# Splitting a layer norm and a router's choice into steps for later slots of an attention loop

## The chip, the cores and the metric

The kernel runs on one core of one Trainium2 chip. Its time is the device time of one execution in microseconds; the times given are medians of several executions.

## The reference

A block of attention and a mixture of experts, each with a residual and a layer norm without weights, in float32. There are four batches of 1024 tokens with 256 features.

```python
x = layernorm(x + attention(x))       # 16 heads of 64, rotary embedding, causal softmax
raw = softmax(x @ gate)               # 16 experts
top3 = top_k(raw, 3)                  # gates of the three, divided by their sum
x = layernorm(x + sum over top3 of gate * (relu(x @ W1[e] + b1[e]) @ W2[e] + b2[e]))
```

## The kernel before

**Attention.** One loop (L428) runs over 32 pairs of heads, n = 0 to 31, eight pairs to a batch, with two turns more to drain. Each pair has six slots, k = 0 to 5. A slot is written (n,k) here. A slot takes one or two blocks of 128 queries, the longest rows first (L411: blocks 7, 6, 5, 4, then 3 and 2, then 1 and 0). For each slot:

- TensorE (PE) computes scores `s` (L300); VectorE (DVE) copies them out of PSUM with the mask and a running minimum (L308, a custom operation that writes `p` and `nmax`); ScalarE (ACT) takes the exponential (L323); DVE inverts the sums (L337, `rinv`); GpSimd (POOL) divides (L340).
- DVE transposes `p` in blocks of 32 (L357, `t_first` and `t_last`); PE multiplies it with the values (L378, `y_ps`); ACT adds a bias (L391); PE applies the output weights (L400, `oo`); DVE adds this to the batch's residual `acc` (L468).
- For the next pair, PE projects queries and keys (L215, `pp`), DVE multiplies by the sine (L220, `rotq` and `rotk`), ACT copies with the bias (L226, `rawq`, `rawk`), DMAs swap halves (L234, `swq`, `swk`), and POOL finishes the rotation (L240, L245). Values of a later pair are `vv` (L254).

Two rules set the order. PE's order is the order of the program text (`tc.manual_schedule`). On the other engines a scheduler places each instruction by when it reckons its inputs ready, within data dependencies and some pairs that are tied by hand (`after`). The PSUM tiles `s`, `pp`, `vv`, `oo` and those of the router come in turn from one pool of four buffers, `ps_s`.

**Norm and router.** When slot (8b+1, 1) has been written, the sums of batch b-1 are complete, and `normalise(b - 1)` (L508) calls `layernorm`: eight statistics (L75), eight aggregations (L77), one square root on ACT (L79), one reciprocal (L81), eight scalings (L83), and then the DMAs that write the batch to x_a, x_b and sums[0] and zeros to sums[1]. `router.batch` returns four steps, a `place` step and 24 scatters. These go through `plan`, a table from (n,k) to functions that are called at the end of that slot's text:

```python
for i, go in enumerate(steps):
    plan[n + i // 2, (3, 5, 1, 3)[i]] = [go]
plan[n + 2, 3] = [place]
```

The steps are `turn(0)` (PE transposes four blocks of tokens, L598, copied out on DVE, L600, and ACT, L602), `logits(0)` (L609, copied at L613), `turn(1)` and `logits(1)`. At the end of `logits(1)`, `choose` follows at once: a softmax over 16 experts (L620 to L627), three rounds that each pick the largest (L635 to L647), and the gates (L649 to L657). All are small DVE operations, except for one exponential on ACT (L623). `place` counts tokens per expert with two matmuls (L667) and turns the counts into row numbers with some 17 DVE operations (L671 to L691); the scatters (L695, POOL) write token numbers and gates into a table by these rows. After batch 2 a first list of tiles is made from the table's counts (L716 to L836), so that experts can start.

**Experts.** After the loop, `moe` runs over tiles of 256 rows, each of one expert: gathers, two layers of matmuls (L896, L912), scatters with addition (L926). The last batch's norm comes at its start, and its router steps go beside tiles through the table `side`. A last norm ends the kernel.

Of the kernel before, what the change touches and what calls it, by code (L numbers as in the profile page):

```python
# [29 lines left out]
FP = mybir.dt.float32  # L30
I32 = mybir.dt.int32
AF = mybir.ActivationFunctionType
ALU = mybir.AluOpType
AX = mybir.AxisListType
# [3 lines left out]
P = 128  # L38
# [5 lines left out]
TC = T // P  # L44
NG = T // 512
NT = B * T
E, TOPK, FF = 16, 3, 512
# [22 lines left out]
def layernorm(nc, pool, acc, c0, n, eps_t):  # L70

    stats = pool.tile([P, n, 6], FP, tag=f"ln_stats{n}")
    mv = pool.tile([P, n, 2], FP, tag=f"ln_mv{n}")
    for i in range(n):
        nc.vector.bn_stats(stats[:, i, :], acc[:, c0 + i, :])  # L75
    for i in range(n):
        nc.vector.bn_aggr(mv[:, i, :], stats[:, i, :])  # L77
    std = pool.tile([P, n], FP, tag=f"ln_std{n}")
    nc.scalar.activation(std, mv[:, :, 1], AF.Sqrt, bias=eps_t)  # L79
    rstd = pool.tile([P, n], FP, tag=f"ln_rstd{n}")  # L80
    nc.vector.reciprocal(rstd, std)  # L81
    for i in range(n):
        nc.vector.tensor_scalar(  # L83
            acc[:, c0 + i, :], acc[:, c0 + i, :], mv[:, i, 0:1], rstd[:, i : i + 1],
            ALU.subtract, ALU.mult,
        )


def attention(
# [4 lines left out]
    nc = tc.nc  # L94
    with ExitStack() as ctx:
# [6 lines left out]
        rp = pool("a_rope", 1)  # L102
# [8 lines left out]
        sp = pool("a_small", 4)  # L111
# [8 lines left out]
        xts, accs = {}, {}  # L120
# [58 lines left out]
            ), "divide")  # L179

        def normalise(b, small):
            layernorm(nc, small, accs[b], 0, TC, eps_t)
            for d in ([x_a] if b < B - 1 else []) + [x_b, sums[0]]:
                nc.sync.dma_start(
                    out=d[ds(b * T, T)].rearrange("(c p) d -> p c d", p=P), in_=accs[b]
                )
            late(nc.sync.dma_start(
                out=sums[1][ds(b * T, T)].rearrange("(p c) d -> p (c d)", p=P)
                .rearrange("p (k n) -> p k n", n=512),
                in_=zero.unsqueeze(1).to_broadcast([P, T * D // (P * 512), 512]),  # L190
            ))
# [170 lines left out]
        st = {}  # L362
# [58 lines left out]
        plan = {}  # L421
# [5 lines left out]
        with tc.manual_schedule(engines={mybir.EngineType.PE}):  # L427
            for n in range(n_pairs + 2):  # L428
                b, p = divmod(n, NP)
                if n == 2:  # L430
                    load_router()
                for k in range(n_slots):
# [72 lines left out]
                    for go in plan.pop((n, k), []):  # L505
                        go()
                    if k == 1 and p == 1 and 0 < b < B:
                        normalise(b - 1, sp)  # L508
                        steps, place, scatters = router.batch(
                            b - 1, accs[b - 1], ps_s, "s", ps_s, "s"  # L510
                        )
                        for i, go in enumerate(steps):
                            plan[n + i // 2, (3, 5, 1, 3)[i]] = [go]
                        plan[n + 2, 3] = [place]
                        for i in range(3):
                            for slot, c0, c1 in ((0, 0, 2), (1, 2, 4), (5, 4, 8)):
                                plan[n + 3 + i, slot] = scatters[8 * i + c0 : 8 * i + c1]
                        if b == B - 1:
                            plan[n + 6, 1] = [lambda: first.extend(router.first_list())]
                            plan[n + 6, 3] = [  # L520
                                lambda: first[1](router.on_dve), lambda: first[2](ps_s, "s")
                            ]
# [11 lines left out]
class Router:  # L534
# [48 lines left out]
    def batch(self, b, acc, ps_t, t_tag, ps_p, p_tag):  # L583
# [6 lines left out]
        def bc(t):  # L590
            return t.unsqueeze(2).to_broadcast(full)

        def turn(tb):
            t = rp.tile([P, DC, 512], FP, tag="x2T", name="x2T")
            for c in range(DC):
                ps = ps_t.tile([P, 512], FP, tag=t_tag, name="x2_ps")
                for u in range(4):
                    nc.tensor.transpose(ps[:, ts(u, P)], acc[:, tb * 4 + u, ts(c, P)], self.ident)  # L598
                if c % 2:
                    nc.vector.tensor_copy(t[:, c, :], ps)  # L600
                else:
                    nc.scalar.copy(t[:, c, :], ps)  # L602
            st["x2T"] = t

        def logits(tb):
            ps = ps_p.tile([P, 4, E], FP, tag=p_tag, name="lg_ps")
            for u in range(4):
                for c in range(DC):
                    nc.tensor.matmul(  # L609
                        ps[:, u, :], lhsT=st["x2T"][:, c, ts(u, P)], rhs=self.gate_sb[:, c, :],  # L610
                        start=(c == 0), stop=(c == DC - 1),
                    )
            nc.vector.tensor_copy(lg[:, ts(tb, 4), :], ps)  # L613
            if tb == 1:
                choose()

        def choose():

            m = rp.tile([P, TC], FP, tag="m", name="m")
            nc.vector.tensor_reduce(m, lg, AX.X, ALU.max)  # L620
            nc.vector.tensor_tensor(lg, lg, bc(m), ALU.subtract)
            pr = rp.tile(full, FP, tag="pr", name="pr")
            nc.scalar.activation(pr, lg, AF.Exp)  # L623
            s = rp.tile([P, TC], FP, tag="s", name="s")
            nc.vector.tensor_reduce(s, pr, AX.X, ALU.add)
            nc.vector.reciprocal(s, s)
            nc.vector.tensor_tensor(pr, pr, bc(s), ALU.mult)  # L627
            gr = rp.tile([P, TOPK, TC], FP, tag="gr", name="gr")
            tmp = rp.tile(full, FP, tag="tmp", name="tmp")
            picks = rp.tile(full, FP, tag="picks", name="picks")  # L630
            hots = []
            rank_b = self.consts["rank"].unsqueeze(1).to_broadcast(full)
            for r in range(TOPK):
                hot = rp.tile(full, FP, tag=f"hot{r}", name=f"hot{r}")
                nc.vector.tensor_reduce(m, lg, AX.X, ALU.max)  # L635
                nc.vector.tensor_tensor(hot, lg, bc(m), ALU.is_equal)
                nc.vector.tensor_tensor(hot, hot, rank_b, ALU.mult)
                nc.vector.tensor_reduce(m, hot, AX.X, ALU.max)
                nc.vector.tensor_tensor(hot, rank_b, bc(m), ALU.is_equal)
                if r == 0:  # L640
                    nc.vector.tensor_copy(picks, hot)
                else:
                    nc.vector.tensor_tensor(picks, picks, hot, ALU.add)
                if r < TOPK - 1:
                    nc.vector.scalar_tensor_tensor(lg, hot, -3e38, lg, ALU.mult, ALU.add)
                nc.vector.tensor_tensor(tmp, hot, pr, ALU.mult)
                nc.vector.tensor_reduce(gr[:, r, :], tmp, AX.X, ALU.add)  # L647
                hots.append(hot)
            nc.vector.tensor_tensor(s, gr[:, 0, :], gr[:, 1, :], ALU.add)  # L649
            nc.vector.tensor_tensor(s, s, gr[:, 2, :], ALU.add)  # L650
            nc.vector.tensor_scalar_max(s, s, GATE_EPS)
            nc.vector.reciprocal(s, s)
            pair = rp.tile([P, TOPK, TC, 2], FP, tag="pair", name="pair", bufs=2)
            nc.vector.tensor_tensor(
                pair[:, :, :, 1], gr, s.unsqueeze(1).to_broadcast([P, TOPK, TC]), ALU.mult
            )
            nc.vector.tensor_copy(  # L657
                pair[:, :, :, 0],
                self.consts["tok"][:, ts(b, TC)].unsqueeze(1).to_broadcast([P, TOPK, TC]),
            )  # L660
            st.update(m=m, tmp=tmp, picks=picks, hots=hots, pair=pair)

        def place():

# [29 lines left out]
        def scatter(c, r):  # L694
            i = nc.gpsimd.indirect_dma_start(  # L695
                out=self.table,
                out_offset=bass.IndirectOffsetOnAxis(ap=st["slots"][:, r, c : c + 1], axis=0),
                in_=st["pair"][:, r, c, :], in_offset=None,
            )
            tc.declare_no_dep(  # L700
                i.ins, group=f"scatter{b}", reason="the entries of two scatters differ"
            )
            tc.add_to_no_dep_group(f"scatter{b}", i.ins)

            tc.add_manual_dep(
                i.ins, self.behind.ins.name, NO_SYNC, reason="issue order"
            )

        return [
            lambda: turn(0), lambda: logits(0), lambda: turn(1), lambda: logits(1),  # L710
        ], place, [lambda c=c, r=r: scatter(c, r) for c in range(TC) for r in range(TOPK)]

    def count(self):
# [116 lines left out]
def moe(tc, router, first, last_norm, acc, ident, eps_t, wall, x_a, x_b, sums, out):  # L830
    nc = tc.nc
    with ExitStack() as ctx:
# [101 lines left out]
                before = s  # L934

        steps, place, scatters = router.batch(B - 1, acc, ps_t, "t", ps_r, "r")
        side = {1: steps[:1], 2: steps[1:3], 3: steps[3:], 5: [place]}
        for i, go in enumerate(scatters):
            side.setdefault(6 + i // 8, []).append(go)
        later = []  # L940
# [190 lines left out]
```

## Time and profile before

| | |
|---|---|
| median of 3 executions | 1741.03 us (1738.7 to 1745.79) |
| the profiled execution | 1742.73 us |
| its span, first to last instruction | 1740.8 us |
| mean granted TensorE clock | 0.969 |
| attention loop | to about 1250 us |
| experts | to about 1690 us |

The profile is of one execution, and the rows' times are of it. An instruction's duration on DVE can overlap with its successor's start, so what a row of small operations takes is read from start to start. "Granted clock" is the share of TensorE's full speed that the chip allowed in a stretch. "[1.59 <-DVE nmax L308]" behind a row says that the engine had been idle for 1.59 us before it, and that a DVE instruction of line 308 ended the wait. In an answer by windows the columns are: the window, its length, and busy us (and instructions) of PE, PE's weight loads, DVE, ACT and POOL, then granted clock, busy share of the DMA engines, and GB/s.

### The profile page before, as it was taken

What the parts mean: (1) busy time and instruction counts of PE and PEld (TensorE: products, weight loads), DVE (VectorE), ACT (ScalarE), POOL (GpSimd) and SP (SyncE); (2) the same over time, 40 slices, a digit from 0 to 9 for tenths busy, and PEclk for the clock granted to TensorE, in tenths of its full rate; (3) what the DMA queues carried; (4) which work ended last, traced back from release to release, by engine and by line L of the source; (5) the groups of instructions that cost most, each with busy time, mean ns of one, the idle gap of its engine ahead of it and who ended that gap; (6) DMA issues with size and microseconds to landing.
All of it is one profiled execution on the core that took longest, in us unless ns stands there. A gap on an engine that the chain in (4) does not pass through costs nothing. (4 is left out here: it accounts for less than half of the span.)

```text
span 1740.8 us, 51881 instructions
## 1 busy us (share of the span) xinstructions
PE 1606.5 (92%) x20920; PEld 1097.8 (63%) x20920; DVE 1169.2 (67%) x3516; ACT 716.2 (41%) x1634; POOL 1106.4 (64%) x1050
## 2 busy tenths in 40 slices
PE   7899999989899998989999898999899999999970
PEld 3556556656556565655655565565588888888860
DVE  4678878888888788888887888888655222222224
ACT  3445445544444455445454554454322222222214
POOL 2656565754468865646786454588557778888544
PEclk9999999999999999999999999999899999999995
DMA  6454644464355546535554553444668998989857
GB/s 186 110 144 123 166 120 123 120 198 110 93 134 142 127 111 187 126 83 141 128 144 117 145 154 96 102 119 103 206 202 191 227 241 245 246 238 245 215 96 268
DMA packets 118166, 272.96 MB, mean 157 GB/s; under 512 B 21873, under 2 KB 72433, under 8 KB 102562
## 3 DMA queue, kind: packets, MB, share of 16 engines
q1 hardware_dynamic: 93122, 239.91, 49.8%
q0 software_dynamic: 24656, 29.68, 9.4%
q8 instruction: 167, 2.74, 0.7%
q14 instruction: 77, 0.63, 0.1%
q10 hardware_dynamic: 144, 0.01, 0.0%
HBM read 183.17 MB, written 52.79 MB: 136 GB/s over the span
## 5 line engine op out<-in xcount | busy, mean ns | idle before, releaser
L340 POOL TENSOR_SCALAR p<-p,rinv 128x512 f32<-128x512 f32 (+7 forms) x512 | 374.8, 747 | 436.0 <-DVE rinv L337 432.0
L323 ACT ACTIVATE p<-p,nmax 128x512 f32<-128x512 f32 (+7 forms) x512 | 391.9, 766 | 468.3 <-DVE nmax L308 446.9
L300 PE MATMUL s<-rotk,rotq 64*128 64x512 f32 (+3 forms) x1536 | 338.1, 522 | 21.9 <-POOL rotq L245 10.3
L357 DVE STREAM_TRANSPOSE t_first<-p 128x512 f32<-128x512 f32 (+3 forms) x512 | 276.7, 583 | 26.9 <-PE y_ps L378 26.3
L215 PE MATMUL pp<-xT,wqk 128*128 128x512 f32 x512 | 258.6, 630 | 35.8 <-DVE nmax L308 20.5
L300 PEld LDWEIGHTS s<-rotk,rotq 64*128 64x128 f32 x1536 | 152.7, 188 | 172.2 <-issue 96.9
L378 PEld LDWEIGHTS y_ps<-t_first,vr 32*64 32x64 f32 x8192 | 164.6, 133 | 101.3 <-DVE t_first L357 31.3
L378 PE MATMUL y_ps<-t_first,vr 32*64 32x160 f32 (+1 forms) x8192 | 222.0, 346 | 4.0 <-DVE t_first L357 3.8
L308 DVE CUSTOM_DVE_ANT_0 p<-s,zero 128x512 f32<-128x512 f32 x256 | 165.6, 683 | 87.6 <-PE s L300 87.6
L901 ACT ACTIVATE hid<-ps,w 128x256 f32<-128x256 f32 x224 | 93.9, 470 | 314.6 <-issue 252.2
L917 DVE TENSOR_TENSOR y<-ps,w 128x512 f32<-128x512 f32 x56 | 38.7, 691 | 274.5 <-PE ps L912 274.5
L926 POOL DMA_INDIRECT sums<-y,ids x112 | 178.4, 1592 | 69.1 <-DVE y L922 37.8
L896 PE MATMUL ps<-xg,w 128*128 128x256 f32 x896 | 204.4, 382 | 2.7 <-DVE xg L886 2.7
L912 PE MATMUL ps<-w,hid 128*128 128x256 f32 x896 | 202.6, 379 | 0.0
L912 PEld LDWEIGHTS ps<-w,hid 128*128 128x128 f32 x896 | 169.9, 190 | 22.9
L896 PEld LDWEIGHTS ps<-xg,w 128*128 128x128 f32 x896 | 167.1, 191 | 23.7 <-DVE xg L886 2.9
L215 PEld LDWEIGHTS pp<-xT,wqk 128*128 128x128 f32 x512 | 92.2, 195 | 130.7 <-issue 67.2
L378 PEld LDWEIGHTS y_ps<-t_last,vr 32*64 32x64 f32 x7424 | 113.7, 133 | 79.4 <-issue 64.4
L400 PE MATMUL oo<-wo,yT 128*128 128x256 f32 x512 | 147.1, 412 | 6.4 <-DVE nmax L308 4.6
L378 PE MATMUL y_ps<-t_last,vr 32*64 32x96 f32 (+3 forms) x7424 | 139.5, 253 | 3.3 <-ACT yT L391 0.6
L308 DVE CUSTOM_DVE_ANT_0 p<-s,mask,nmax 128x512 f32<-128x512 f32 (+3 forms) x256 | 130.3, 546 | 0.9 <-issue 0.5
L254 PE MATMUL vv<-wv,xT 128*128 128x256 f32 x512 | 121.3, 380 | 4.8 <-DVE nmax L308 4.8
(147 smaller groups left out, 1890.3 us busy)
## 6 DMA issues: line engine op xcount, KB each, us to landing
vr<-v_d SPq DMA_DIRECT2D x256, 256.0 KB
w<-in_wall_dram SPq DMA_DIRECT2D x56, 1154.0 KB
swk<-rawk SPq DMA_DIRECT2D x128, 128.0 KB
swq<-rawq SPq DMA_DIRECT2D x256, 64.0 KB
v_d<-v SPq DMA_DIRECT2D x128, 128.0 KB
wqk<-in_w_qk_dram SPq DMA_DIRECT2D x32, 256.0 KB
xT<-in_xT_dram SPq DMA_DIRECT2D x8, 512.0 KB
wv<-in_w_v_dram SPq DMA_DIRECT2D x16, 256.0 KB
```

Of the source, the lines that this page charges most:

```text
L215: nc.tensor.matmul(ps, lhsT=wqk[n][:, c, i, :], rhs=xts[b, g][:, c, :], start=(c == 0), stop=(c == DC - 1),)
L254: nc.tensor.matmul(ps[:, u, :], lhsT=xts[b, cc // 2][:, c, ts(cc % 2 * 2 + u, P)], rhs=wv[n][:, c, :], start=(c == 0), stop=(c == DC - 1),)
L300: nc.tensor.matmul(s[:, :n_k], lhsT=rot[n, 0, qc // 4][ts(hh, KD), ts(qc % 4, P)], rhs=k[ts(hh, KD), ds(k0, n_k)], start=True, stop=True,)
L308: i = nc.vector.tensor_tensor_reduce(out=probs[n, qc, hh][:, ds(k0, n_k)], in0=s[:, :n_k], in1=mask[:, 512 - n_k :] if last else zero[:, : ...
L323: nc.scalar.activation(pr, pr, AF.Exp, bias=m, scale=-1.0, accum_out=rsum[:, hh : hh + 1])
L340: order["divide"] = router.behind = nc.gpsimd.tensor_scalar(pr, pr, rinv[:, hh : hh + 1], 1.0, ALU.mult, ALU.mult)
L357: order["turn"] = router.on_dve = after(nc.vector.transpose(turned[n][h][:, hh, :, ds(i - 4 * h, n_j, step=7 - 4 * h), :], probs[n, i, hh] ...
L378: nc.tensor.matmul(st[n][a][ts(hh, KD), ds(32 * j, 32 * (TC - j))], lhsT=vrs[n, h][ts(a, 32), jh // 2 * 8 + 2 * u + jh % 2, ts(hh, KD)], r ...
L400: nc.tensor.matmul(ps[:, v, :], lhsT=st[n][:, ts(2 * h + v, P)], rhs=wo[n], start=True, stop=True,)
L896: nc.tensor.matmul(ps[:, f - f0, :], lhsT=w[:, ds(c * FF + f * P, P)], rhs=xg[:, c, :], start=(c == 0), stop=(c == DC - 1),)
L912: nc.tensor.matmul(ps[:, h, :], lhsT=hid[:, f, ts(h, P)], rhs=w[:, ds(W2_AT + f * D, D)], start=(f == 0), stop=(f == FC - 1),)
L926: s = behind(nc.gpsimd.indirect_dma_start(out=sums[t % 2], out_offset=bass.IndirectOffsetOnAxis(ap=ids[:, h, i : i + 1], axis=0), in_=y[:, ...
```

## The change

`layernorm` no longer runs at once; it returns four functions: statistics of the first half of the token blocks, statistics of the second half with the square root, reciprocal and scaling of the first half, scaling of the second half. In the loop the first is called in slot (n,1), and the others go into `plan` for (n,2), (n,3) and (n,4), the last with the DMAs. The choice becomes four functions as well: softmax and first pick, second pick, third pick, gates. The router's steps are entered for later slots: transposes and logits at (n,5), (n+1,1), (n+1,3), (n+1,5), the choice at (n+2,1) to (n+2,4), and `place` at (n+2,5) instead of (n+2,3). The scatters keep their slots. In `moe` the norm runs as one, and the choice is split between tiles 3 and 4. No operation is added, removed or resized.

```diff
+    def take(i0):
+        for i in range(i0, i0 + n // 2):
+            nc.vector.bn_stats(stats[:, i, :], acc[:, c0 + i, :])
+        for i in range(i0, i0 + n // 2):
+            nc.vector.bn_aggr(mv[:, i, :], stats[:, i, :])
+        if i0:
+            nc.scalar.activation(std, mv[:, :, 1], AF.Sqrt, bias=eps_t)
+
+    def scale(i0):
+        if i0 == 0:
+            nc.vector.reciprocal(rstd, std)
+        for i in range(i0, i0 + n // 2):
+            nc.vector.tensor_scalar(
+                acc[:, c0 + i, :], acc[:, c0 + i, :], mv[:, i, 0:1], rstd[:, i : i + 1],
+                ALU.subtract, ALU.mult,
+            )
+
+    return [lambda f=f, i0=i0: f(i0) for f in (take, scale) for i0 in (0, n // 2)]
...
                     if k == 1 and p == 1 and 0 < b < B:
-                        normalise(b - 1, sp)
+                        norm = layernorm(nc, sp, accs[b - 1], 0, TC, eps_t)
+                        norm.append(lambda b=b: keep(b - 1))
+                        norm[0]()
                         steps, place, scatters = router.batch(
                             b - 1, accs[b - 1], ps_s, "s", ps_s, "s"
                         )
+                        plan[n, 2] = norm[1:2]
+                        plan[n, 3] = norm[2:3]
+                        plan[n, 4] = norm[3:]
                         for i, go in enumerate(steps):
-                            plan[n + i // 2, (3, 5, 1, 3)[i]] = [go]
-                        plan[n + 2, 3] = [place]
+                            plan[n + min((i + 2) // 3, 2), (5, 1, 3, 5, 1, 2, 3, 4)[i]] = [go]
+                        plan[n + 2, 5] = [place]
...
             nc.vector.tensor_copy(lg[:, ts(tb, 4), :], ps)
-            if tb == 1:
-                choose()
...
         return [
             lambda: turn(0), lambda: logits(0), lambda: turn(1), lambda: logits(1),
+            choose, lambda: pick(1), lambda: pick(2), gates,
         ], place, [lambda c=c, r=r: scatter(c, r) for c in range(TC) for r in range(TOPK)]
...
         steps, place, scatters = router.batch(B - 1, acc, ps_t, "t", ps_r, "r")
-        side = {1: steps[:1], 2: steps[1:3], 3: steps[3:], 5: [place]}
+        side = {1: steps[:1], 2: steps[1:3], 3: steps[3:6], 4: steps[6:], 5: [place]}
```

`keep` holds the DMAs that stood in `normalise`; `choose` ends with `pick(0)`, and `pick` and `gates` hold the lines of the old `choose` unchanged.

## The prediction

> **What bounds the kernel now.** I read the page's busy shares first, then the timeline of VectorE (DVE) for the start of each slot, then busy time by window, then PE's own timeline for its idle gaps.
>
> ```profile
> PE 1606.5 (92%) x20920; PEld 1097.8 (63%) x20920; DVE 1169.2 (67%) x3516; ACT 716.2 (41%) x1634; POOL 1106.4 (64%) x1050
> ```
>
> TensorE (PE) leads, but shares over the span mix attention with experts. So, by pair of heads (us; the first figure after the window is its length; the last but two is the granted clock):
>
> ```profile
> 557.30:593.10 35.80, 35.38 (x592) 21.71 (x597) 29.39 (x90) 18.27 (x42) 29.42 (x30) 1.00 0.51 124
> 354.10:398.00 43.90, 39.24 (x606) 25.00 (x605) 35.72 (x108) 21.63 (x46) 22.02 (x24) 0.96 0.68 194
> 398.00:442.50 44.50, 39.58 (x612) 24.89 (x610) 38.94 (x127) 19.40 (x44) 21.04 (x21) 0.98 0.41 99
> 442.50:485.50 43.00, 39.00 (x599) 23.71 (x604) 35.88 (x108) 18.27 (x42) 21.51 (x22) 0.94 0.40 97
> 1019.60:1064.40 44.80, 39.88 (x622) 24.66 (x626) 39.06 (x128) 19.39 (x44) 21.06 (x21) 1.00 0.39 97
> 1064.40:1108.40 44.00, 39.66 (x596) 23.10 (x598) 39.46 (x130) 18.38 (x42) 21.55 (x22) 0.96 0.39 96
> ```
>
> The first is pair 14, a quiet one: PE busy 35.38 of 35.80 us, DVE 29.39. Pairs 9, 10, 11 carry norm and router of batch 0 and take 131.4 us, where three quiet ones take 107.5: 23.9 us extra. Batch 1 (17 to 19) has 131.2, batch 2 (25 to 27) 43.9 + 44.8 + 44.0 = 132.7, or 25.2 extra. These 73 us are all that the change can touch. In them PE waits for DVE; its timeline in pair 10, slots 4 and 5, shows for what:
>
> ```profile
> 429.54 1.99 PE L254 MATMUL vv<-wv,xT 128*128 128x256 f32 x8 [1.59 <-DVE nmax L308]
> 433.67 1.98 PE L215 MATMUL pp<-xT,wqk 128*128 128x512 f32 x4 [1.28 <-DVE acc L468]
> 438.72 1.44 PE L300 MATMUL s<-rotk,rotq 64*128 64x512 f32 x4 [1.03 <-DVE nmax L308]
> 440.74 2.66 PE L300 MATMUL s<-rotk,rotq 64*128 64x512 f32 x4 [0.59 <-ACT rawq L226]
> ```
>
> Scores, `pp`, `vv`, `oo` and the router's tiles share a ring of four PSUM buffers (ps_s). Each waits until the tile four before it is read, by DVE (L308, L468, L220) or ScalarE (L226). Router work put ahead of those reads stops PE.
>
> **The change, part by part.** *Norm.* I compared the built order of both kernels. DVE's is the same up to the first x2T copy of batch 0: the scheduler, which goes by readiness, had already put the statistics into slots (8,3) to (9,0), and the eight scalings still follow the reciprocal in one row at (9,0) and (9,1). ScalarE's square root has its old place too. So the norm keeps its cost: slots (9,0) and (9,1) take 13.2 + 7.1 us against 6.35 + 7.6 in a quiet pair, 6.4 us a batch. On SP's queue the x_a, x_b and sums writes stay where they were; only the zeroing of sums[1] goes behind four swq copies: nothing, since no rotation waits for swq after the first pair (17.1 us, once, is all). POOL's order is identical.
>
> What is left to the router in each batch is then 23.9 - 6.4 = 17.5 us (batches 0 and 1), and 25.2 - 6.4 = 18.8 (batch 2, with the first list's arithmetic).
>
> *Transposes and logits* move from (9,3), (9,5), (10,1), (10,3) to (9,5), (10,1), (10,3), (10,5). PE's rows: 1.04 us for eight transposes, 1.85 us for logits; less an overlap of about 0.15 each, 5.2 us. Quiet slots hold PE gaps of 0.55 (L300 for rawk) and 0.35 (L215), which absorb some: (9,3) to (10,2) grew by 2.5 us where 3.5 us of PE work went in. I take 4.3 us (3.5 to 5.2).
>
> *The choice.* In the built order it isn't spread over four slots. Of its ops, 34 stand in (11,0): twelve between the transposes L357 and the sum L468, 22 after rotk (L220); three small ones follow in (11,1). Before, they were threaded through (10,3) to (10,5). Durations, start to start:
>
> ```profile
> 424.63 0.29 DVE L620 TENSOR_REDUCE m<-lg 128x8 f32<-128x128 f32 x1
> 424.95 0.87 DVE L621 TENSOR_TENSOR lg<-lg,m 128x128 f32<-128x128 f32 x1
> 425.75 0.68 DVE L308 CUSTOM_DVE_ANT_0 p<-s,mask 128x512 f32<-128x512 f32 x1
> ...
> 427.32 1.35 DVE L627 TENSOR_TENSOR pr<-pr,s 128x128 f32<-128x128 f32 x1
> 428.60 0.28 DVE L637 TENSOR_TENSOR hot<-hot,rank 128x128 f32<-128x128 f32 x1
> ...
> 477.52 0.28 DVE L689 TENSOR_TENSOR tmp<-hot,slot 128x128 f32<-128x128 f32 x1
> 477.83 0.29 DVE L690 TENSOR_REDUCE m<-tmp 128x8 f32<-128x128 f32 x1
> 478.15 0.17 DVE L691 CAST slots<-m 128x8 int32<-128x8 f32 x1
> ```
>
> First twelve: 0.32 + 0.80 (L620, L621) + 1.28 (L627) + 0.46 (L636) + eight of 0.11 to 0.21 = 4.3 us. The later 22: an op behind an unrelated one starts 0.20 us after it, one that reads its neighbour's result 0.31 us (the last three rows). Eight are of the second kind, eleven of the first, three small: 2.5 + 2.2 + 0.4 = 5.1 us.
>
> The trace has a slot that also follows logits: (10,0).
>
> ```profile
> 400.59 1.30 DVE L357 STREAM_TRANSPOSE t_first<-p 128x512 f32<-128x512 f32 x2
> 401.81 0.65 DVE L468 TENSOR_TENSOR acc<-oo,acc 128x512 f32<-128x512 f32 x1
> 402.39 1.02 DVE L357 STREAM_TRANSPOSE t_first<-p 128x384 f32<-128x384 f32 x2
> 403.33 0.12 DVE L337 RECIPROCAL rinv<-rsum 128x2 f32<-128x2 f32 x1
> 403.37 0.73 DVE L220 SCALAR_TENSOR_TENSOR rotk<-pp,bqk,sin 128x512 f32<-128x512 f32 x1
> 405.15 0.69 DVE L308 CUSTOM_DVE_ANT_0 p<-s,zero 128x512 f32<-128x512 f32 x1 [1.04 <-PE s L300]
> ```
>
> Laid over it: the sum starts at 406.1 instead of 401.8 and ends at 406.7, rotk at 408.4, rawk (0.69) at 409.1. PE, at its next scores (404.0), needs the sum's buffer for the third tile (idle 1.8 us) and rawk's for the fourth (1.9). It goes on to 411.2; its `pp` needs the first score reduction of (11,1), which starts at 408.4 + 5.1 = 413.5: idle 2.9 us, to 414.1. The product behind it needs transposes ready at 413.5 + 2.3 + 0.2 + 0.7 = 416.7, where the template has 409.1. The choice costs PE 7.6 us. Bounds: 4.5, if DVE's idle time of (10,0) to (10,2), 4.7 us, takes its full share of 9.4 us; 9.4, if nothing does. I take 7.6, since the wait at the fourth score tile is in the trace already: PE's weight load there waits 0.6 us for rawk in 31 slots, so nothing in slot 0 hides a later rotk. Behind the waiting PE stand all products of the pair; ScalarE and POOL have slack.
>
> Here a rule can be weighed. The rows give 0.31 us for a chained op against 0.20. "VectorE: DVE Perf Modes" of the Trainium skill, section on the DRAIN, says that ops chained by semaphores take as long as unchained ones; by that the 22 would take about 0.9 us less in each batch, 2.7 in all.
>
> *Half speed.* After such gaps the granted clock falls: 0.50 in 369.1:372.5, 0.51 in 440.7:447.6, 0.50 in 1099.5:1102.9, each behind gaps of 1.0 to 3.5 us that add up to about half of the 3.4 us before. Pair 11's slot 0 took 9.1 us after the dip of 6.9 us; pair 27's, with none, 6.3: a dip costs up to 2.8 us. The new gaps (1.8, 1.9, 2.9 within 9 us) are larger, but PE waits through part of the dip: I take 2.2 us (0 to 3.4).
>
> On that, "TensorE: Matmul & The Clock Gate" of the Trainium skill, Part 1, puts the fall behind an idle window of about 3.4 us. By that rule the gaps below would bring no dip and the sum would be 9 us less; the dip at 1099.5, behind gaps of 1.54 and 2.04 us, speaks against it.
>
> *Placing* moves from (11,3)-(11,4), where it cost 2.9 + 3.2 - 1.2 = 4.9 us, to (11,5)-(12,0). Two copies and the scan (0.2 + 0.2 + 2.1) now delay the first score reduction of (12,0); the rest, 4.3 us, lies between its reductions and ahead of the sum and rotk. Laid over pair 15's slot 0 in the same way: PE idle 0.5, 1.1, 0.2, 2.6 (the product needs the transposes) and 1.5 (rawk): with 0.5 for its two matmuls, less its own 0.2, 6.2 us (bounds 2.8, with DVE's idle time as cover, and 7.3, with none), and 0.8 for a dip (0 to 1.7). The first scatter stands behind a division that needs rinv, which DVE computes after the slots: no new wait on POOL. In batch 2 the first list adds 21 small ops behind rotk of (28,0), 3.7 us by their rows at 1100.4 to 1106.5: 2.5 us on PE, so 8.7.
>
> *Experts:* DVE waits 274.5 us for PE there; the choice fits in tiles 3 and 4 as it did in 3. Nothing.
>
> **Sum.** After, batches 0 and 1: 4.3 + 7.6 + 2.2 + 6.2 + 0.8 = 21.1, against 17.5: +3.6 each. Batch 2: 4.3 + 7.6 + 2.2 + 8.7 + 0.8 = 23.6 against 18.8: +4.8. Together +12.0 us. On the profiled execution (1742.73 us; span 1740.8) 1754.7; it lay 1.7 us above the median 1741.03, so 1753. From no change, 0.5% (8.7 us) is about what a measurement can tell.
>
> **Rivals.**
> - *DVE's idle time covers the bursts.* Slots 0 to 2 idle 4.5 to 4.7 us on DVE, slots 4 and 5, where the work was, 1.9. If PE needs neither sum nor rotk early, the choice costs 9.4 - 4.7 = 4.7, placing 6.8 - 4.5 + 0.5 = 2.8, no dip: 11.8 against 17.5, twice; batch 2 with 3.7 more, 15.5 against 18.8. -14.7 us: 1726. It decides if PE's scores of slot 1 start without a gap; the 31 waits for rawk speak against.
> - *Only the place changes.* The stalls are as computed, but no dip follows: 18.1 and 20.6 against 17.5 and 18.8, +3.0: 1744.
> - *Longer half-speed stretches:* two windows at each of six places, 3.4 us each instead of 2.2 and 0.8: +11.4 more, 1764. For: 440.7:447.6. Against: 369.1 lasted one.
> - *The norm isn't moved* is no rival but in the sum: had it been spread, its 6.4 us would be at stake three times.
>
> **Chances.** Forecast 0.60, cover 0.12, place only 0.18, long stretches 0.10. Range: 1738 (place only, at its low bounds) to 1764; the cover is outside, with half of the long stretches. The forecast's own range is 1746 to 1762. Faster by over 0.5%: 0.12; within: 0.18 and 0.06 of the forecast's low end, 0.24; slower 0.64.
>
> **What would show it.** Right: slots (9,0), (17,0), (25,0) still 13 us; (10,3) to (10,5) quiet but for logits; (11,0), from its first score reduction to the next slot's, about 15 us instead of 7 to 9, PE idle there for acc, rawk and nmax; (11,5) over 8 and (12,0) about 10. Wrong: PE without gaps at (11,1), or a shorter (9,0).

## The result, and the profile after

| | before | after |
|---|---|---|
| median of 8 executions | 1742.13 us (1738.7 to 1745.79) | 1750.94 us (1748.09 to 1758.76) |
| the profiled execution | 1742.73 us | 1748.09 us |
| its span | 1740.8 us | 1746.2 us |
| mean granted TensorE clock | 0.969 | 0.964 |

The change costs 8.8 us: a ratio of 1.0067, with a 95% interval of 1.0051 to 1.0082. In the rows below, line numbers of after are 12 to 23 above those of before: scores are L312, their reduction L320, transposes L369, products L390, the sum L480, rotk and rotq L232, the choice L635 to L680, the placing L694 to L714. Shares of the whole span show nothing:

```profile
PE 1609.0 (92%) x20920; PEld 1096.8 (63%) x20920; DVE 1167.4 (67%) x3516; ACT 715.8 (41%) x1634; POOL 1106.2 (63%) x1050
```

The table by pairs does. This is the answer by windows for after: pairs 9, 10, 11 and 12 of batch 0, pairs 25, 27 and 28 of batch 2, and the quiet pair 14.

```profile
352.80:395.70 42.90, 38.24 (x590) 23.89 (x587) 35.41 (x107) 21.74 (x46) 21.80 (x23) 0.96 0.69 196
395.70:435.40 39.70, 39.28 (x625) 26.35 (x626) 30.49 (x93) 18.78 (x43) 21.64 (x24) 1.00 0.47 116
435.40:482.20 46.80, 39.72 (x591) 23.12 (x588) 40.65 (x129) 18.52 (x43) 21.36 (x23) 0.89 0.35 86
482.20:520.90 38.70, 36.78 (x594) 22.21 (x601) 31.96 (x104) 18.28 (x42) 25.05 (x25) 1.00 0.55 138
976.80:1020.60 43.80, 40.02 (x590) 24.25 (x590) 35.47 (x109) 21.74 (x46) 21.85 (x24) 0.88 0.68 195
1060.20:1107.00 46.80, 39.94 (x591) 23.42 (x590) 40.65 (x128) 18.52 (x43) 21.39 (x23) 0.89 0.36 87
1107.00:1152.90 45.90, 39.29 (x594) 22.87 (x596) 38.97 (x127) 18.28 (x42) 24.93 (x25) 0.93 0.37 91
556.70:592.60 35.90, 35.48 (x592) 21.82 (x600) 29.43 (x91) 18.29 (x42) 29.44 (x30) 1.00 0.52 124
```

Pair 10 fell from 44.5 to 39.7 us: the choice has left it. Pair 11 rose from 43.0 to 46.8, and its clock fell to 0.89; pair 12, quiet before, now takes 38.7. The four pairs of a batch together took 167.3, 167.2 and 168.6 us before, and 168.0, 167.6 and 176.1 after: +0.7, +0.4 and +7.5. So the loss is nearly all in batch 2, whose pair 28 carries the placing and the first list at once. (The spans of these two executions differ by only 5.4 us, less than the 8.6 of the three batches: after was 1.3 us shorter ahead of pair 9 and 1.6 us shorter behind the loop.)

PE's own timeline of slot (11,0) shows the burst of 34 choice operations from the side of the engine that waits:

```profile
444.97 0.91 PE L312 MATMUL s<-rotk,rotq 64*128 64x384 f32 x2 [1.45 <-ACT rawk L238]
452.91 3.78 PE L227 MATMUL pp<-xT,wqk 128*128 128x512 f32 x4 [4.84 <-DVE nmax L320]
```

PE waits 1.45 us for rawk and 4.84 us for the first score reduction of (11,1), which stands behind the burst on DVE. Then 446.5:456.8 runs at half speed. The slot takes 16.8 us where a quiet one takes 6.35.

### The profile page after: what moved, and what is told of

Read it like the earlier page. It is cut to its first block, busy times and chain, and to the rows that moved or that the text cites. A ratio compares the mean times of both kernels' runs of the same rounds, so it can differ in the third digit from the quotient of the medians.

```text
span 1746.2 us, 51887 instructions
## 1 busy us (share of the span) xinstructions
PE 1609.0 (92%) x20920; PEld 1096.8 (63%) x20920; DVE 1167.4 (67%) x3516; ACT 715.8 (41%) x1634; POOL 1106.2 (63%) x1050
## 3 DMA queue, kind: packets, MB, share of 16 engines
q8 instruction: 167, 2.74, 0.7%
## 5 line engine op out<-in xcount | busy, mean ns | idle before, releaser
L312 PE MATMUL s<-rotk,rotq 64*128 64x512 f32 (+3 forms) x1536 | 336.1, 517 | 26.5 <-ACT rawk L238 13.6
L227 PE MATMUL pp<-xT,wqk 128*128 128x512 f32 x512 | 265.1, 643 | 42.9 <-DVE nmax L320 37.7
L369 DVE STREAM_TRANSPOSE t_first<-p 128x512 f32<-128x512 f32 (+3 forms) x512 | 276.9, 583 | 26.5 <-PE y_ps L390 25.9
L312 PEld LDWEIGHTS s<-rotk,rotq 64*128 64x128 f32 x1536 | 150.6, 187 | 178.8 <-issue 94.9
L390 PEld LDWEIGHTS y_ps<-t_first,vr 32*64 32x64 f32 x8192 | 166.7, 135 | 104.9 <-issue 31.3
L390 PE MATMUL y_ps<-t_first,vr 32*64 32x160 f32 (+1 forms) x8192 | 225.8, 350 | 5.0 <-DVE t_first L369 3.6
L320 DVE CUSTOM_DVE_ANT_0 p<-s,zero 128x512 f32<-128x512 f32 x256 | 165.9, 682 | 88.3 <-PE s L312 88.3
L941 DVE TENSOR_TENSOR y<-ps,w 128x512 f32<-128x512 f32 x56 | 38.7, 692 | 275.4 <-PE ps L936 275.3
L390 PEld LDWEIGHTS y_ps<-t_last,vr 32*64 32x64 f32 x7424 | 112.5, 131 | 77.4 <-issue 62.3
L390 PE MATMUL y_ps<-t_last,vr 32*64 32x96 f32 (+3 forms) x7424 | 138.2, 250 | 3.4 <-ACT yT L403 0.6
L320 DVE CUSTOM_DVE_ANT_0 p<-s,mask,nmax 128x512 f32<-128x512 f32 (+3 forms) x256 | 130.9, 546 | 0.7 <-PE s L312 0.4
```

Source lines behind the costliest of these rows:

```text
L227: nc.tensor.matmul(ps, lhsT=wqk[n][:, c, i, :], rhs=xts[b, g][:, c, :], start=(c == 0), stop=(c == DC - 1),)
L312: nc.tensor.matmul(s[:, :n_k], lhsT=rot[n, 0, qc // 4][ts(hh, KD), ts(qc % 4, P)], rhs=k[ts(hh, KD), ds(k0, n_k)], start=True, stop=True,)
L320: i = nc.vector.tensor_tensor_reduce(out=probs[n, qc, hh][:, ds(k0, n_k)], in0=s[:, :n_k], in1=mask[:, 512 - n_k :] if last else zero[:, : ...
L369: order["turn"] = router.on_dve = after(nc.vector.transpose(turned[n][h][:, hh, :, ds(i - 4 * h, n_j, step=7 - 4 * h), :], probs[n, i, hh] ...
L390: nc.tensor.matmul(st[n][a][ts(hh, KD), ds(32 * j, 32 * (TC - j))], lhsT=vrs[n, h][ts(a, 32), jh // 2 * 8 + 2 * u + jh % 2, ts(hh, KD)], r ...
```

## The experiments

Three theories were told apart. **A, place:** a burst of DVE work costs what it delays of the reads that PE waits for (the sum, rotk, the next score reduction), so the same operations are cheap elsewhere. **B, amount:** DVE's added work costs its own length wherever it stands. **C, GpSimd:** the length of a DVE burst depends on what GpSimd does beside it. Every ratio is against the kernel before on the same chip; a quiet pair's six slots take 6.35, 7.6, 6.1, 4.8, 5.1 and 5.9 us.

**1. The norm's steps alone** (the new `layernorm` and `plan` entries for it; the router's steps, `choose` and `place` as before).

> The norm in four steps as in the kernel after, the router as in the kernel before. Theory A (the built order decides): the norm's scalings stay in one row at (9,0) and (9,1), so these slots take 13.2 + 7.1 us as before, and the time is 1742 us, ratio 1.000 (0.9985 to 1.0015). Rival (the norm's steps carry a part of the 8.7 us, by the write of zeros on SP's queue or by other waits): ratio 1.002 or more.

1742.33 us, ratio 1.0005 (0.9991 to 1.0019). Slots (9,0) and (9,1) took 13.2 and 7.3 us. The norm's half of the change does nothing.

**2. The router's steps alone.**

```diff
-                        norm = layernorm(nc, sp, accs[b - 1], 0, TC, eps_t)
-                        norm.append(lambda b=b: keep(b - 1))
-                        norm[0]()
+                        normalise(b - 1, sp)
...
-                        plan[n, 2] = norm[1:2]
-                        plan[n, 3] = norm[2:3]
-                        plan[n, 4] = norm[3:]
```

> The router as in the kernel after, the norm issued at once as in the kernel before. Theory A: all of the change's cost is here, 1750.5 us, ratio 1.0050 (1.004 to 1.007), slot (11,0) 16.8 us. Rival (both halves of the change are needed): ratio at most 1.003.

1749.84 us, ratio 1.0058 (1.0043 to 1.0073); (11,0) took 16.8 us. Within the noise, all of the cost is here.

**3. GpSimd moved away from the burst.**

```diff
-                    if k == 0 and one_of(n):
+                    if k == (n in (11, 19, 27)) and one_of(n):
                         rotate(n, 0, 0)
```

> The kernel after, with GpSimd's rotation of the second half of q in pairs 11, 19 and 27 one slot later, so that GpSimd's two operations of 1.30 and 1.26 us at 445.9 to 448.6 no longer lie beside the 22 later choice operations of slot (11,0). DVE's order is that of after. Theory C (DVE operations with two SBUF operands wait while GpSimd works): the operations that took 0.8 to 1.25 us there take 0.28 to 0.4, the 22 take 5.4 to 6.7 us instead of 8.05, slot (11,0) 14.2 to 15.5 us instead of 16.8, and the total falls by 4 to 7 us to 1744 to 1747. Rival (number of operations and their chaining alone set the length): slot (11,0) stays 16.5 to 17, total 1750 to 1751.

1744.11 us, ratio 1.0020 (1.0005 to 1.0036), 5.7 us below experiment 2 on the same chip, which has after's order on PE, DVE and GpSimd; (11,0), (19,0) and (27,0) took 15.15 us each instead of 16.8. From the timelines of GpSimd and DVE in after, the GpSimd rows that were moved, and two DVE rows; the second is one of the 22 later operations, the first the same kind of operation a little earlier with GpSimd idle:

```profile
445.93 1.30 POOL L252 TENSOR_TENSOR swq<-swq,cos 128x512 f32<-128x512 f32 x1
447.30 1.26 POOL L257 TENSOR_TENSOR rotq<-rotq,swq 128x512 f32<-128x512 f32 x1
...
441.01 0.28 DVE L642 TENSOR_TENSOR pr<-pr,s 128x128 f32<-128x128 f32 x1
446.13 1.24 DVE L657 TENSOR_TENSOR hot<-hot,rank 128x128 f32<-128x128 f32 x1
```

The operation of 1.24 us began just after GpSimd's first and ended 0.14 us after that one's end at 447.23. With the rotation moved, the same operation and PE's wait behind the burst read:

```profile
447.58 0.29 DVE L657 TENSOR_TENSOR hot<-hot,rank 128x128 f32<-128x128 f32 x1
452.72 3.78 PE L227 MATMUL pp<-xT,wqk 128*128 128x512 f32 x4 [2.84 <-DVE nmax L320]
```

Theory C holds: the 22 operations took 6.4 us instead of 8.05, and PE's wait fell from 4.84 to 2.84. (Two of them, of 0.86 and 0.81 us, still stand beside GpSimd's division of 128x1024.) In a profile this waiting hides as busy time: the row gets longer, and no idle time is shown ahead of it. "SBUF — State Buffer" of the Trainium skill, section "SBUF: two separate sides", has a rule for it: a DVE operation with two SBUF inputs and a GpSimd operation that reads SBUF share a port that the first one holds for its whole instruction. The rows agree, down to the end of the wait.

**4. The choice really in four slots.** The scheduler had put all steps into (11,0), so each step's first operation is tied behind a DVE operation of its own slot.

```diff
+                    router.pin = lambda i: after(i, "part" if k < 2 else "inverse")
                     for go in plan.pop((n, k), []):
                         go()
+                    router.pin = lambda i: i
...
-            nc.vector.tensor_reduce(m, lg, AX.X, ALU.max)
+            self.pin(nc.vector.tensor_reduce(m, lg, AX.X, ALU.max))
```

(and in the same way the first operation of `pick(1)`, `pick(2)` and `gates`)

> The kernel after, with the first operation of each of the choice's four steps tied behind the last reciprocal (or rotk) of its own slot, so that DVE has 14 choice operations at the end of (11,1), 9 among the reductions of (11,3), 9 of (11,4), 4 of (11,5), and none in (11,0). The other work is where it was. Theory A (the place of the burst, ahead of the sum and of rotk in slot 0, makes the cost): (11,0) falls from 16.8 to 6.5-7 us, slots (11,0) to (11,5) together cost 5 to 6.5 us over a quiet pair instead of about 10, and the total is 1738 (1735 to 1741). Rival B (DVE's added work counts, 10.7 us of it in 39 operations, wherever it stands): slots (11,0) to (11,5) cost 9.5 to 10.5 as before, only shifted, total 1749 to 1752.

1745.90 us, ratio 1.0031 (1.0018 to 1.0044): 4 us better than experiment 2 on the same chip, where theory A wanted 9 to 15. (11,0) to (11,5) took 7.1, 8.6, 6.3, 9.75, 7.2 and 5.4 us. The 14 operations at the end of (11,1) cost only 1.0 us, but the nine in (11,3) cost 5.0. DVE's and GpSimd's timelines there:

```profile
460.92 1.71 DVE L664 TENSOR_TENSOR hot<-rank,m 128x128 f32<-128x128 f32 x1
463.04 2.00 DVE L668 TENSOR_TENSOR picks<-picks,hot 128x128 f32<-128x128 f32 x1
...
460.09 2.38 POOL L252 TENSOR_TENSOR swk<-swk,cos 128x1024 f32<-128x1024 f32 x1
462.55 2.34 POOL L257 TENSOR_TENSOR rotk<-rotk,swk 128x1024 f32<-128x1024 f32 x1
```

Two operations of 0.28 us took 1.71 and 2.00, ending 0.16 and 0.15 us after GpSimd's. So place counts (A), and GpSimd's work beside a place takes its gain away (C). In a quiet pair GpSimd's long two-operand instructions stand in slots 1, 3 and 4. In pair 16 of after those of slot 1 run from 1.4 to 4.0 us into it; behind rotk, at the end of slot 1, a division is left, and in slot 2 nothing. In a pair with scatters they come later: in pair 14 the second runs from 5.1 to 6.4 us into slot 1.

**5 to 8. Four changes one by one.** These ran on another chip, where the kernel before took 1809.16 us and no ratio differs from 1 within ±0.4%. In the profile of the kernel with the later placing, 42 us of the extra time lie behind (31,5), and most of the rest in slot 0 of pairs 13 to 15, 21 to 23 and 29 to 31, which take 8.9 to 10.0 us there instead of 6.35. These are the slots in which GpSimd issues four scatters each. PE waits there for nothing that the profile names: on that page the group of first products has 22.9 us of idle time, most of it "issue", where the page of before has 4.0.

```profile
L378 PE MATMUL y_ps<-t_first,vr 32*64 32x160 f32 (+2 forms) x8192 | 255.6, 351 | 22.9 <-issue 18.0
```

So these four settle nothing by their totals, and only rows of slots without such gaps are read.

Choice tied where GpSimd is idle:

```diff
-                            plan[n + min((i + 2) // 3, 2), (5, 1, 3, 5, 1, 2, 3, 4)[i]] = [go]
+                            a, c = ((0, 2), (0, 3), (0, 4), (0, 5), (1, 1), (1, 2), (2, 1), (2, 2))[i]
+                            plan.setdefault((n + a, c), []).append(go)
```

> The kernel after, with the router's transposes and logits in slots 2 to 5 of pair n (9, 17, 25), and the choice tied into slots in which GpSimd is idle: 14 operations behind rotk of (10,1), nine behind rotq of (10,2), eight behind rotk of (11,1), six behind rotq of (11,2). The norm and the placing are those of after. Theory A + C (a burst costs little where no read that TensorE waits for stands close behind it and GpSimd doesn't work beside it): 14 operations cost 1.0 us, as they did at (11,1) of the kernel with the tied choice (8.6 against 7.6 us), the nine 1.5 (2.4 us of work in 0.9 us of idle time), the rest at most 0.9; about 3.4 us a batch instead of about 10, and a total of 1731 (1727 to 1736). Rival B (DVE's added work counts wherever it stands): 39 operations of 0.2 to 0.3 us, 9 us a batch, 1746 to 1750.

(Here the transposes stand ahead of the norm's scaling in the program, so the router reads rows that are not yet scaled.) 1804.94 us, ratio 0.9980 (0.9939 to 1.0021). (10,1) took 10.0, (10,2) 8.0 (with a half-speed stretch from 420.3), (11,1) 8.3 and (11,2) 6.2 us: 5.1 us for the choice, more than the 3.4 expected, but half of the 10 in after.

First list tied behind rotk of (29,1):

```diff
+                                router.late_list = order["part"]     # called in slot (n + 4, 1)
...
+            self.tc.add_manual_dep(i.ins, self.late_list.ins.name, NO_SYNC, reason="issue order")
```

> The kernel after, with the arithmetic of the first list (24 small operations of one batch) tied behind rotk of (29,1) instead of standing behind rotk of (28,0), where the placing is too. Theory A: slot (28,0) falls from 15.8 to 8.6 us, as in the other batches, (29,1) grows from 7.6 to 8.6-9.4, net 5.4 to 6.2 us less, total 1745. Rival B (work counts, 3.7 us): net 3.5 us or less.

1805.01 us, ratio 0.9998 (0.9961 to 1.0035). (28,0) fell to 8.6 us, but (29,1) and (29,2) took 10.5 and 7.8, where the kernel of the last experiment of this group has 7.9 and 6.1: net 2.9 us gained. That lies within what theory B allowed (3.5 or less), but doesn't show it: 1.7 of the 4.3 us lost in pair 29 are those of (29,2), where the clock is at half speed from 1193.2 on. The 24 operations, most of 0.17 us, took 4.6 us on DVE (1187.6 to 1192.2), the first of them 1.06 us beside a division, and slot 1 has cover for a little over 2 (the 14 of experiment 4, 3.4 us long, cost 1.0).

Norm's scalings tied:

```diff
-            nc.vector.reciprocal(rstd, std)
+            pin(nc.vector.reciprocal(rstd, std))           # pin: behind rotk of (n,1)
...
+            if i >= n // 2:
+                pin(m)                                     # the second four: behind rotq of (n,2)
```

> The kernel after, with the norm's eight scalings really spread: the reciprocal and four of them tied behind rotk of (9,1), four behind rotq of (9,2); also in pairs 17 and 25. Theory A: (9,0) falls from 13.2 to 7-7.6 us, (9,1) takes 7.6-8.5, (9,2) 7-7.6; the norm costs 1.5 to 3 us a batch instead of 6.4, 10 to 15 us less in all, total 1738 (1735 to 1741). Rival B (work counts): 4 us of scalings and 2.4 us of statistics stay 6 us a batch, total 1749 to 1751.

1801.76 us, ratio 0.9989 (0.9944 to 1.0033). (9,0), (9,1) and (9,2) took 7.7, 8.4 and 6.4 us, the same in pairs 17 and 25: 22.5 instead of 26.5, so the norm costs 2.45 us instead of 6.4. Theory A.

Placing alone moved, in the kernel before:

```diff
-                        plan[n + 2, 3] = [place]
+                        plan[n + 2, 5] = [place]
```

> The kernel before, with only the placing moved from slot 3 to slot 5 of pair n + 2, as in the change. Theory C (the placing was dear at (11,3) because GpSimd worked beside it, and is cheap at (11,5) to (12,1)): placing costs 3.5 us instead of 4.9 in batches 0 and 1; in batch 2 the first list follows it into (28,0), where both cost 10.9 instead of 8.3: -1.4 - 1.4 + 2.6 = 0, total 1741 (1739 to 1743). Rival (the prediction's own term, 7.0 us for the placing and 9.5 with the list): +2.1 + 2.1 + 1.2, total 1747.

1804.44 us, ratio 0.9983 (0.9944 to 1.0022). (11,3) to (11,5) fell back to 4.8, 5.1 and 6.7 us, and (12,0) took 8.6, as in after. (12,1) took 9.6 us, 1.5 more than in after: here half speed followed the placing, from 490.3 to 493.7.

**9 and 10. All of it together, and without the norm.** The norm's scalings tied as above; transposes and logits at (9,3) to (10,0); `pick(1)` and `pick(2)` cut in halves, so that the choice has 14 operations at (10,1), 4 at (10,2), 9 at (11,1), 10 at (11,2); the list in two parts, tied at (28,1) and (29,1). The other kernel leaves the norm to the scheduler.

```diff
+                            a, c = ((0, 3), (0, 4), (0, 5), (1, 0), (1, 1), (1, 2), (2, 1), (2, 1), (2, 2), (2, 2))[i]
+                            plan.setdefault((n + a, c), []).append(go)
...
+                            for a in (3, 4):
+                                plan.setdefault((n + a, 1), []).append(here)
```

> The kernel after with everything really spread over slots 1 and 2, behind rotk and rotq, where GpSimd is idle most of the time: the norm's scalings four behind rotk of (9,1) and four behind rotq of (9,2); transposes and logits at (9,3), (9,4), (9,5), (10,0); the choice as 14 operations at (10,1), 4 at (10,2), 9 at (11,1), 10 at (11,2); the placing as in after; the first list's arithmetic in two parts behind rotk of (28,1) and (29,1). Theory A + C: the norm costs 2.5 us a batch (as in the kernel with the tied norm: 7.7, 8.4, 6.4 us in its three slots, 22.5 against 26.5) instead of 6.4; the choice 3 to 4 instead of 10; the list 1.5 to 2.5 instead of 7.4. That is 3 x (3.9 + 6.5) + 5.4 = 36 us less than after: 1714 to 1715 (1708 to 1724) where the kernel before takes 1741, ratio 0.985 (0.980 to 0.991). Rival B (DVE's added work counts wherever it stands): 1741 to 1751, ratio 1.000 to 1.006.

> The same, but the norm's scalings left to the scheduler as in the change, so that they stand in one row at (9,0) and (9,1). Theory A: 3 x 3.9 = 12 us more than the kernel with everything tied: 1726 (1719 to 1735), ratio 0.992 (0.988 to 0.996), slots (9,0) + (9,1) 20 us. Rival (the norm's row is hidden once the router is out of the way): no more than 3 us above it.

All tied: **1724.55 us, ratio 0.9914 (0.9887 to 0.9940)**, faster than both kernels. Norm left alone: 1738.56 us, ratio 0.9995 (0.9978 to 1.0013), 14 us slower than all tied (12 were expected), with (9,0) and (9,1) again at 13.2 and 7.2. Both totals lie above what was expected for them, the first by a little. Pairs 9 to 12 of the kernel with everything tied, by windows:

```profile
353.30:394.70 41.40, 38.73 (x614) 25.36 (x614) 35.69 (x111) 22.22 (x47) 21.88 (x24) 1.00 0.66 181
394.70:434.70 40.00, 37.74 (x611) 23.60 (x613) 33.99 (x108) 18.51 (x43) 20.91 (x21) 1.00 0.51 133
434.70:473.20 38.50, 36.18 (x587) 22.40 (x588) 34.72 (x114) 18.28 (x42) 22.07 (x24) 1.00 0.45 111
473.20:511.80 38.60, 36.68 (x594) 22.12 (x601) 31.93 (x104) 18.28 (x42) 25.01 (x25) 1.00 0.54 139
```

DVE does the same work, but batch 0 takes 158.5 us instead of 168.0, with the full clock throughout. Batches 1 and 2, with four half-speed stretches of 3.4 us, take 160.4 and 165.5, where before took 167.2 and 168.6. The choice costs 1.0 + 0.2 + 0.8 + 1.0 = 3.0 us ((10,1) 8.6, (10,2) 6.3, (11,1) 8.4, (11,2) 7.1) instead of 10.15. The gain was less than expected at two places: the second logits stand in slot 0, where they cost 3.0 us ((10,0) took 9.4), and the list cost 5.7 us instead of 1.5 to 2.5, (28,1) alone 11.6. That holds a half-speed stretch behind the placing; (20,1), with such a stretch and no list, took 9.6.

**11. GpSimd made busy beside the placing,** by multiplications of a scratch tile that nothing uses.

```diff
+                            for i in range(5):
+                                m = nc.gpsimd.tensor_tensor(extra, extra, extra, ALU.mult)
+                                if i == 0:
+                                    after(m, "divide")
+                            place()
```

> The kernel after with added GpSimd work beside the placing: five multiplications of a scratch tile, 128x512 each (about 1.3 us, two operands in SBUF), behind the last division of (11,5), (19,5) and (27,5), where GpSimd had been idle for 7 us. DVE's and TensorE's order stay. Theory C (the placing is cheap in after because GpSimd doesn't work beside it): the placing's operations with two SBUF operands take up to 1.3 us instead of 0.28 to 0.48, five waits of 0.7 to 1.2 us, slot (12,0) takes 10.5 to 13 us instead of 8.6, the placing about 6 to 8 us instead of 3.5, and the total rises by 5 to 12 us to 1756 to 1763. Rival D (the placing is cheap by its place among the score reductions): (12,0) stays 8.6 to 9.0, total 1750 to 1752.

1754.64 us, ratio 1.0083 (1.0069 to 1.0096). Beside the 1.0067 of after, on another chip, that is not clear of the noise, so the rows have to tell. (12,0), (20,0) and (28,0) grew by 1.4 to 1.5 us, to 10.0, 10.0 and 17.3. That is theory C, at a price below the 10.5 expected for (12,0) and the 1756 for the whole, since GpSimd's five instructions took 1.1 us each and mostly their remainder was waited for. (12,1) and (20,1), now at half speed, rose from 8.1 and 8.0 to 9.6, but slots of 9.6 us stand behind the placing in experiments 8, 9, 10 and 12 as well, without the added work, so this part is not shown to be GpSimd's. Even an operation on 16 columns, 0.18 us in after, waits (GpSimd and DVE):

```profile
484.90 5.56 POOL L535 TENSOR_TENSOR extra<-extra 128x512 f32<-128x512 f32 x5
485.22 0.76 DVE L712 TENSOR_TENSOR shift<-at,tot 128x16 f32<-128x16 f32 x1
```

**12. Logits out of slot 0, list two pairs later.**

```diff
-                            a, c = ((0, 3), (0, 4), (0, 5), (1, 0), (1, 1), (1, 2), (2, 1), (2, 1), (2, 2), (2, 2))[i]
+                            a, c = ((0, 2), (0, 3), (0, 4), (0, 5), (1, 1), (1, 2), (2, 1), (2, 1), (2, 2), (2, 2))[i]
...
-                            for a in (3, 4):
+                            for a in (4, 5):
```

> The kernel with everything tied, with the transposes and logits one slot earlier (9,2) to (9,5), so that no logits stand in slot 0, where they cost 3.0 us ((10,0) 9.4 instead of 6.35), and the first list's two parts at (29,1) and (30,1) instead of (28,1) and (29,1), where they met the placing's last slot. Theory A + C: transposes and logits 4.3 us a batch instead of 6.1, so 5.5 us less in all; the list 3 us instead of 6; the total 8 us less, 1716 (1711 to 1720), ratio 0.986 (0.983 to 0.990). Rival B: 1724, ratio 0.991.

1725.40 us, ratio 0.9918 (0.9905 to 0.9931): a miss, no better than the kernel with everything tied. Transposes and logits fell from 6.2 to 5.2 us in batch 0, but the list rose to 9.8 ((29,1) 11.8, (30,1) 10.1, and a half-speed window in the slot after each). The rows of DVE and GpSimd show why:

```profile
1138.70 2.74 DVE L780 CAST full<-int 128x16 f32<-128x16 int32 x1
1180.50 2.44 DVE L814 TENSOR_TENSOR blk<-blk,step 128x1 f32<-128x1 f32 x1
...
1139.41 2.00 POOL L354 TENSOR_SCALAR p<-p,rinv 128x896 f32<-128x896 f32 x2
1180.93 2.00 POOL L354 TENSOR_SCALAR p<-p,rinv 128x896 f32<-128x896 f32 x2
```

Two operations of about 0.17 us took 2.74 and 2.44, one of them a copy of a single operand, and ended 0.03 and 0.01 us after GpSimd's divisions. So most of what the list cost here is theory C's and not its length's: these pairs hold scatters, which put GpSimd's rotation and division later in slot 1, beside the list. Both operations had begun before the division, while GpSimd was at a scatter; what held them until then is not shown.

## Why the prediction was right, and where its sum was off

1753 us was predicted and 1750.94 measured. The sign and the main stall were as forecast, and the built order told which half of the change would act. The spread over the batches was not: +3.6, +3.6 and +4.8 us were summed, +0.7, +0.4 and +7.5 measured, so errors of opposite sign stand behind the near total, and that it came so near is luck. Of the signs that were named, (11,5) over 8 and (12,0) about 10 us failed: they took 6.7 and 8.6. For batch 0, in us over quiet pairs:

| step | predicted | measured |
|---|---|---|
| norm, (9,0) and (9,1) | 6.4 | 6.4 |
| transposes and logits, (9,3) to (10,5) | 4.3 | 4.45 |
| choice with half speed, (11,0) to (11,2) | 7.6 + 2.2 | 10.15 |
| placing with half speed, (11,5) to (12,1) | 6.2 + 0.8 | 3.55 |

- **Norm.** Right: not moved by the scheduler, and shown by experiment 1. In batch 2 a half-speed stretch of 10.3 us (3.4 before) added 1.0.
- **Choice.** The sum is right, its parts are not. The first twelve operations took 2.7 us, not 4.3, as GpSimd was idle beside them (436.3 to 443.7); the 22 later ones took 8.05, not 5.1. Both came from one mistake: durations were taken from rows of before without asking what GpSimd did beside those. The row "427.32 1.35 DVE L627" that the prediction showed is such a wait: the same operation takes 0.28 us in after. Experiment 3 took 1.65 us of the second error away.
- **The wait that PE shows.** Four waits were laid out, 1.8 + 1.9 + 2.9 us and one for transposes; PE had two, 1.45 and 4.84. The wait for the sum's buffer did not appear, as the first twelve operations were short; the wait for the first score reduction was longer, as the 22 were long.
- **Placing.** The mis-sized term: 7.0 against 3.55 (3.45 in batch 1). PE idles 0.23 and 1.50 us in (12,0), and the scan, counted at 2.1 us from before, took 0.48:

```profile
481.79 0.48 DVE L698 TENSOR_TENSOR_SCAN upto<-tot,zeros 128x128 f32<-128x128 f32 x1
```

  Here GpSimd has only short divisions until 483.3 and then nothing until 490.4. Experiment 8 shows that it is the place and not the rest of the change; experiment 11 that work of GpSimd beside it brings a part of the cost back. That no dip follows in batches 0 and 1, where 0.8 us was counted, is luck by these runs: behind a (12,0) or (20,0) of the same 8.6 us, half speed came in (12,1) of experiment 8, in both slots of experiment 10 and in (20,1) of experiments 9 and 12.
- **Batch 2.** Predicted +4.8 over before, measured +7.5: (27,5) to (28,1) cost 10.9 against 9.5, as the first list's operations too had GpSimd beside them (one on 15 columns, L776, took 1.75 us in after and 0.17 in the kernel with the tied list), and the norm's dip came on top.
- **Half speed.** The forecast one dip behind (11,0) came as a stretch of 10.3 us, and was within the sum. The window before it, 443.1 to 446.5, has PE busy for 1.95 of 3.40 us, with no gap over 1.45 us. A window of before in which PE was no busier, with a gap of 1.59 us, kept the full clock and was followed by it. The rows are two of after and two of before:

```profile
443.10:446.50 3.40, 1.95 (x36) 0.99 (x42) 3.37 (x8) 0.69 (x1) 2.79 (x3) 1.00 0.66 143
446.50:456.80 10.30, 5.46 (x60) 2.31 (x51) 9.26 (x35) 2.16 (x4) 2.14 (x3) 0.50 0.00 0
...
427.10:430.50 3.40, 1.80 (x8) 1.25 (x8) 3.40 (x10) 1.17 (x5) 2.82 (x3) 1.00 0.98 248
430.50:433.90 3.40, 2.12 (x14) 1.49 (x13) 3.40 (x15) 1.66 (x5) 0.00 (x0) 1.00 0.22 48
```

  "TensorE: Matmul & The Clock Gate" of the Trainium skill, Part 1, puts the fall behind an idle window of about 3.4 us. The fall at 446.5 came without one, so the sum rightly went by the row; but the busy share of the window before does not decide it either, and what does is not shown here.
- **The rivals.** DVE's idle time as cover failed for bursts in slot 0, as forecast, but holds at the end of slot 1, where 14 operations cost 1.0 us. "Only the place changes" is near for the dips behind the placing, which stayed away in batches 0 and 1, by luck as said.
- **The chained operations.** In the burst with GpSimd moved away, an operation that reads its neighbour's result still starts 0.32 us behind it, others 0.20. The prediction went by such rows; "VectorE: DVE Perf Modes" of the Trainium skill, section "The DRAIN you can't avoid", says of its own measurement that a semaphore between operations costs nothing extra, and these small operations differ from that.

## What to carry to other kernels

When work is entered for "a later slot" of a loop that a scheduler orders, look at the built order: without a tie to an operation of that slot the steps run together at the first moment they are ready. Before taking a VectorE duration from a trace, look at GpSimd in the same stretch: a row of a two-operand SBUF operation may be mostly a wait, and the best slot for such work is one where GpSimd is idle and TensorE's next read is far. A slot that is free in one pair need not be so in the next: where scatters had delayed GpSimd, the same slot was dear. Short bursts behind the last read of a slot were nearly free here (14 operations for 1.0 us); a burst longer than the cover, like the first list with its 4.6 us, cost 2.6 us in its slot and brought half speed on top.

## What was not expected of the hardware

- VectorE operations with two SBUF operands that started beside a GpSimd instruction ended 0.14 to 0.16 us after that instruction: 0.28 us became 1.24, 1.71 and 2.00 beside GpSimd instructions of 1.30, 2.38 and 2.34 us. Reductions of one operand in the stretch of the first kept their 0.27 to 0.29 us, but a copy of one operand took 2.74 us in experiment 12.
- The granted clock fell to one half behind a stretch of 3.4 us in which PE was 57% busy, and did not fall behind one in which it was 53% busy.
- On one chip the kernel before took 1809 us where the others gave 1739 to 1742. A kernel profiled there lost the time in the loop mostly in the slots 0 that hold four scatters, a part of it in PE's "issue" gaps, and 42 us behind the loop; what causes either stays open.
